# Three edits to an AdaLN and FFN kernel: one transfer for the small inputs, tap scalings on another engine, and x1's rows written in two later parts

## The chip, the cores and the metric

The kernel runs on one core of a Trainium2 chip. The metric is the device time of one execution in microseconds, as a median of several. A core has a matrix engine (TensorE, PE in the profile; its weight loads are PEld), a vector engine (VectorE, DVE), an activation engine (ScalarE, ACT), a general engine (GpSimd, POOL) and a queue engine (SyncE, SP). Each runs its own list of instructions in order. ACT, POOL and SP also issue the transfers, which 16 DMA engines carry out. Matrix results land in eight PSUM banks.

## The reference, cut to what matters

There are 32 images of 128 channels by 2048 positions. Two residual layers follow each other, `x = x + F0(x)` and `x = x + F1(x)`:

```python
# layer 0: a mixture of 8 1x1 convolutions per image, then a dense 2048x2048 layer with a low-rank update
h   = gelu(gelu(cond @ W0 + b0) @ W1 + b1)
att = softmax(h @ W2 + b2)                          # 32 x 8
y   = einsum('boi,bih->boh', einsum('bk,koi->boi', att, weight), x) + (att @ bias_k)[:, :, None]
x   = x + y @ W.T + bias + lowrank(y)
# layer 1: grouped convolution (4 groups, 9 taps, padding 4), then a block-wise FFN on permuted positions
y   = conv1d(x, w9, groups=4, padding=4) + (cond @ c_weight.T)[:, :, None] + fside[None, :, None]
t   = y.reshape(4096, 2048)[:, perm].reshape(4096, 16, 128)
t   = einsum('bhm,hmd->bhd', gelu(einsum('bhd,hdm->bhm', t, up)), down)
x   = x + t.reshape(4096, 2048)[:, unperm].reshape(32, 128, 2048)
```

All inputs and the result are float32.

## The kernel before

**The dense layer** is computed ahead of the mixture: the product of x with the 2048x2048 matrix comes first, the 128x128 mixtures of each image are applied to its result. It is done in seven rounds (`ROUNDS`, P1, P2, P6, P7, P5, P3, P4: a Strassen-like scheme on quarters of the matrix), each over eight groups `g` of four images. One round and group is one call of `multiply`: seven inner products, each of 4 matmuls (8 records in the profile), on three banks `px`, `py`, `pz`. After each product `add` puts the bank onto an accumulator, by ScalarE where the accumulator is new (L278) and by VectorE else (L276). Several products use the same bank one after the other, so the next product on `px` waits for the `add` of the last. Between two products `between(j)` puts other work into the queues. In round P1 this is the making of the matrix itself from W and the low-rank factors (`w_make`, L167, L171). In rounds P2 to P3 it is the mixing of the kernels of the images (`mixed_kernel`, L356, L358, VectorE). GpSimd makes sums of the inputs and weights for the coming products (L229 to L253, L336, L338).

**The small work** is a generator, `small()`, that is moved on by one piece after each `multiply`. Its first piece (L664 on) comes after the first multiply: ScalarE issues ten transfers of small inputs into one tile `small`, and then those of `perm` into `pos` and of the mixture's weights into `mix`. The following pieces compute the attention over the eight kernels. Later pieces (L770 to L793) transform the 9-tap convolution kernels: VectorE combines the three parts `T0`, `T1`, `T2` of `toep` to six sets of taps, four into `tw` and two in place, and SP stores them.

**The last round (P4) and the FFN** are run as one pipeline of stages `k`. Each `multiply` of the last round holds three stages, between its products; then each of the 128 heads of the FFN (eight groups by 16 heads: `ffn_up` L626, gelu L629, `ffn_down` L637, residual add L642, scatter L644) is one stage. A pair of images `c` takes 12 stages, n = -2 to 9, and a new pair starts every eight stages, so n of one pair is n - 8 of the next:

- n = -2 and 1: `mix_loads` of the pair's first and second image (SP: L365, L368, L373); n = -1 and 2: `mix_bias` (GpSimd: L379)
- n = 0 and 2: `mix_begin` (ScalarE: L387), `mix_work` (PE L396, VectorE L399); then SP moves the new x, called x1, channel group by channel group to two tiles `xg` (L403)
- n = 3: `residual_rows` (VectorE: 16 transposes, L436, into two tiles `x1t`, and two stores of 1024 KB by SP, L409)
- n = 4 and 5: `conv_inputs` (VectorE, L466 to L478) for the first half of the channels, n = 7 and 8 for the second
- n = 5, 6 and 8, 9: the convolution's products (`conv_begin`, `conv_middle`, `conv_end`, PE L487) and the rest of it, with `conv_rows` (8 transposes, L423, and two stores) at n = 6 and 9.

`xg` holds both images of a pair, as index `j`: j = 0 came at stage n = 0, j = 1 at n = 2. The gathers of a group of images (GpSimd, L610) read what `residual_rows` and `conv_rows` stored to `hx_d`. In the list of one stage the loads and biases come first, then `ffn_up`, the middle products, `ffn_down` of the head before, and at the end `stage_third`: products, then `third_rest` with the transposes and the inputs of the convolution. All orders are the program's own (`manual_schedule`). Tiles of 128x2048 come from a pool of 24 slots. Before a transfer by SP or ACT is issued it can have to wait for an earlier one whose semaphore it takes over: eight are dealt out in turn for both queues together.

Of the kernel before, what the change touches and what calls it, by code (L numbers as in the profile page):

```python
# [11 lines left out]
ALU = mybir.AluOpType  # L12
# [4 lines left out]
P = 128  # L17
B = 32
L = 2048
QW = 512  # L20
KEXP = 8
GR = 4
GC = 32
TAPS = 9
NPH = 4
NK = 4
NM = QW // NK
# [8 lines left out]

ROUNDS = ("P1", "P2", "P6", "P7", "P5", "P3", "P4")
# [3 lines left out]
def adaln_ffn_kernel(  # L45
# [1 line left out]
    tc: tile.TileContext,  # L47
    x: bass.AP,
    xT: bass.AP,
    condT: bass.AP,  # L50
    fside: bass.AP,
    W0: bass.AP,
    b0: bass.AP,
    W1: bass.AP,
    b1: bass.AP,
    W2: bass.AP,
    b2: bass.AP,
    mixT: bass.AP,
    bias_kT: bass.AP,
    WT: bass.AP,  # L60
    fbias: bass.AP,
    A: bass.AP,
    BfT: bass.AP,
    coeffs: bass.AP,
    toep: bass.AP,
    cwT: bass.AP,
    ffw: bass.AP,
    perm: bass.AP,
    out: bass.AP,
# [1 line left out]
    nc = tc.nc  # L71
# [271 lines left out]


    ags = {}
    late, ins, pms, xgs, va, vb, hts, open_ = {}, {}, {}, {}, {}, {}, {}, {}

    def mixed_kernel(b, ks):

# [57 lines left out]
    def store(c, o, h, t):  # L407
        g, j = c // 2, c % 2
        nc.sync.dma_start(  # L409
            hx_d[g][:, o, j * 2 * P : (j + 1) * 2 * P].rearrange(  # L410
                "(p h s) t -> p h s t", h=2, s=2 * NM // GC
            )[:, h],
            t.rearrange("p k s j r c -> p (k s) (j r c)"),
        )

    def rows_tile(name):
        return slot(name, (P, 2, NM // GC, 2, GR, GC))
# [7 lines left out]
                v[:, r].rearrange("p j (s c) -> p j s c", c=GC),  # L425
            )

    def residual_rows(c):

        ts = [rows_tile(f"x1t_{c}{h}") for h in range(2)]  # L430
        for j in range(2):
            for h, t in enumerate(ts):
                for k in range(2):
                    for i in range(2):
                        n0 = (2 * h + k) * NM
                        nc.vector.transpose(  # L436
                            t[:, k, :, j, 2 * i : 2 * i + 2].rearrange("p s r c -> p r s c"),
                            xgs[c][i][:, :, j, n0 : n0 + NM].rearrange("p r (s c) -> p r s c", c=GC),
                        )
        for h, t in enumerate(ts):  # L440
            store(c, 1, h, t)

# [141 lines left out]
    def third_rest(c, n):  # L586
        if n in (6, 9):
            conv_rows(c, int(n == 9))
        if n == 3:
            residual_rows(c)  # L590
        if n in (4, 5, 7, 8):
            conv_inputs(c, int(n > 5), n in (5, 8))
        if n == 8:
            xgs.pop(c)

# [70 lines left out]
    def small():  # L666
        sm = slot("small")
        used = [0]

        def load(name, src, rows, cols, eng=nc.scalar):  # L670
            t = sm[0:rows, used[0] : used[0] + cols]
            used[0] += cols
            if src is not None:
                eng.dma_start(t, src)
            return t

        cond_s = load("cond_s", condT, P, B)
        w0 = load("w0", W0, P, P)
        b0s = load("b0s", b0, P, 1)
        w1 = load("w1", W1, P, P)  # L680
        b1s = load("b1s", b1, P, 1)
        w2 = load("w2", W2, P, KEXP)
        b2s = load("b2s", b2.to_broadcast([B, KEXP]), B, KEXP)
        bk = load("bk", bias_kT, P, KEXP)
        cw = load("cw", cwT, P, GR * P)
        fb = load("fb", fside, P, GR)
        nc.scalar.dma_start(pos, perm)
        nc.scalar.dma_start(mix, mixT)
        h0, h1 = load("h0", None, P, B), load("h1", None, P, B)
        lg, ex, att = (load(n, None, B, KEXP) for n in ("lg", "ex", "att"))  # L690
        mx, su, rs = (load(n, None, B, 1) for n in ("mx", "su", "rs"))
        adiag = load("adiag", None, B, B * KEXP)
        ones = load("ones", None, P, P)
        nc.gpsimd.memset(ones, 1.0)
        yield

        p0 = bank()
        nc.tensor.matmul(p0[:, :B], lhsT=w0, rhs=cond_s, start=True, stop=True)
        nc.scalar.activation(h0, p0[:, :B], AF.Gelu, bias=b0s)
        done(p0)  # L700
        yield
        p1 = bank()
        nc.tensor.matmul(p1[:, :B], lhsT=w1, rhs=h0, start=True, stop=True)
        nc.scalar.activation(h1, p1[:, :B], AF.Gelu, bias=b1s)
        done(p1)
        yield
        p2 = bank()
        nc.tensor.matmul(p2[:B, :KEXP], lhsT=h1, rhs=w2, start=True, stop=True)
        nc.vector.tensor_tensor(lg, p2[:B, :KEXP], b2s, ALU.add)
        done(p2)  # L710
        nc.vector.tensor_reduce(mx, lg, AX.X, ALU.max)
        nc.vector.tensor_scalar(lg, lg, mx, None, ALU.subtract)
        nc.scalar.activation(ex, lg, AF.Exp)
        nc.vector.tensor_reduce(su, ex, AX.X, ALU.add)
        nc.vector.reciprocal(rs, su)
        nc.vector.tensor_scalar(att, ex, rs, None, ALU.mult)

        nc.vector.tensor_tensor(
            adiag.rearrange("b (c k) -> b c k", k=KEXP),
            ident.unsqueeze(2).to_broadcast([B, B, KEXP]),  # L720
            att.unsqueeze(1).to_broadcast([B, B, KEXP]),
            ALU.mult,
        )
        yield
        p3 = bank()
        nc.tensor.matmul(p3[:, : B * KEXP], lhsT=ones[0:B], rhs=adiag, start=True, stop=True)
        nc.vector.tensor_copy(att_bc, p3[:, : B * KEXP])
        done(p3)
        ab = att_bc.rearrange("p (b k) -> p b k", k=KEXP)
        nc.vector.tensor_scalar(aggb, ab[:, :, 0], bk[:, 0:1], None, ALU.mult)  # L730
        for k in range(1, KEXP):
            nc.vector.scalar_tensor_tensor(
                aggb, ab[:, :, k], bk[:, k : k + 1], aggb, ALU.mult, ALU.add
            )

        for r in range(GR):
            p4 = bank()
            nc.tensor.matmul(
                p4[:, :B], lhsT=cw[:, r * P : (r + 1) * P], rhs=cond_s, start=True, stop=True
            )  # L740
            nc.vector.tensor_scalar(ctxb[:, r], p4[:, :B], fb[:, r : r + 1], None, ALU.add)
            done(p4)
        nc.vector.tensor_scalar(ctx34, ctxb, 0.75, None, ALU.mult)

        nc.vector.tensor_scalar(row, pos, 3, 9, ALU.bitwise_and, ALU.logical_shift_left)
        nc.vector.tensor_scalar(
            orow[:, 0], pos, 0x1FC, None, ALU.bitwise_and
        )
        nc.vector.tensor_scalar(orow[:, 1], pos, 9, None, ALU.logical_shift_right)
        nc.vector.tensor_tensor(row, row, orow[:, 0], ALU.add)  # L750
        nc.vector.tensor_tensor(row, row, orow[:, 1], ALU.add)
        for g in range(NG):
            nc.vector.tensor_scalar(orow[:, g], pos, g * L, None, ALU.add)
        yield

        while len(made) < 16:
            yield
        wbc = slot("wbc", (P, NPH, QW))
        for o in range(NPH):
            p5 = bank()  # L760
            for half in (slice(0, NQ), slice(NQ, QW)):
                nc.tensor.matmul(
                    p5[:, half], lhsT=ones, rhs=wsum[:, o, half], start=True, stop=True
                )
            nc.scalar.copy(wbc[:, o], p5)
            done(p5)
        nc.sync.dma_start(w1_d, wbc.rearrange("p f n -> p (f n)"))
        yield


        tw, t1 = slot("tw", (P, 4, GR, P)), slot("t1", (P, 4, GR, P))
        nc.sync.dma_start(t1[:, 0:3], toep)
        yield
        yield
        T0, T1, T2 = (t1[:, i] for i in range(3))
        ts, stt = nc.vector.tensor_scalar, nc.vector.scalar_tensor_tensor
        nc.vector.tensor_tensor(tw[:, 1], T0, T2, ALU.add)
        ts(tw[:, 1], tw[:, 1], -1 / 6, None, ALU.mult)
        yield
        stt(tw[:, 0], T1, -1 / 6, tw[:, 1], ALU.mult, ALU.add)  # L780
        stt(tw[:, 1], T1, 1 / 6, tw[:, 1], ALU.mult, ALU.add)
        yield
        stt(tw[:, 3], T2, 4.0, T0, ALU.mult, ALU.add)
        ts(tw[:, 3], tw[:, 3], 1 / 12, None, ALU.mult)
        yield
        stt(tw[:, 2], T1, 1 / 6, tw[:, 3], ALU.mult, ALU.add)
        stt(tw[:, 3], T1, -1 / 6, tw[:, 3], ALU.mult, ALU.add)
        nc.sync.dma_start(tw_d, tw.rearrange("p k r c -> p (k r c)"))
        yield
        ts(T0, T0, 0.25, None, ALU.mult)  # L790
        ts(T1, T2, 4.0, None, ALU.mult)
        nc.sync.dma_start(te_d, t1[:, 0:2].rearrange("p k r c -> p (k r c)"))
        yield  # L793

# [54 lines left out]
    nxt, waiting, ts = {}, {}, {}  # L849
# [6 lines left out]
    for i, (r, g) in enumerate(steps):  # L856
# [17 lines left out]
        if ri == 0:  # L874
            for k in blocks[4 + 2 * g : 6 + 2 * g]:
                t = make(k)
# [6 lines left out]
        elif ri + 1 < len(ROUNDS):  # L883
# [3 lines left out]
            if 2 <= g < 6:  # L887
                k = ((g - 2) // 2, (g - 2) % 2)
# [123 lines left out]
```

## Time and profile before

| | us |
|---|---|
| median of 3 runs | 2667.38 (2661.07 to 2668.86) |
| profiled execution | 2668.65 |
| its span | 2666.5 |
| PE busy | 2632.8 (99%) |
| DVE busy | 1359.2 (51%) |
| POOL busy | 1080.3 (41%) |
| ACT busy | 532.4 (20%) |

The profiled execution took 2.15 us more than its span, and is 1.27 us above the median. PE is busy nearly all the time, at a granted clock of 0.995 over the run; its waits for other engines sum to a little over 20 us. Times in the timeline are counted from the start of the span. A row of the timeline has the start, the time it took, the engine and line, the operation, its tiles (out<-in) and sizes, the number of instructions merged into it, and in brackets how long the engine had been idle before it and what ended the wait.

### The profile page before, as it was taken

To read this page: it belongs to the slowest core of one execution; us is meant where nothing else is said; L and a number is where in the kernel's file an instruction comes from. 1 tells how busy PE (TensorE), PEld (TensorE's weight loads), DVE (VectorE), ACT (ScalarE), POOL (GpSimd) and SP (SyncE) were. 2 spreads that over 40 slices of the span, in tenths; PEclk is the share of its full clock that TensorE was granted. 3 is DMA by queue.
4 is the path that set the end of the run, shared out by engine and by line. 5 is a ranking of instruction groups with operands and counts; after the bars stand their busy time and mean duration, and the time that the engine had idled before them with its cause. 6 is when DMAs were issued, how large, how long until landed. Compare 5 with 4: busy or idle time off the path is not lost.

```text
span 2666.5 us, 19802 instructions
## 1 busy us (share of the span) xinstructions
PE 2632.8 (99%) x6504; PEld 1236.3 (46%) x6504; DVE 1359.2 (51%) x2136; ACT 532.4 (20%) x1099; POOL 1080.3 (41%) x665
## 2 busy tenths in 40 slices
PE   9999999999999999999999999999999999999998
PEld 4444444444444444444444445544555455555543
DVE  6545145233344355454266666666666666566610
ACT  0000100000000000000011144444444444444432
POOL 2544545624636421656242232434332343333222
PEclk9999999999999999999999999999999999999999
DMA  8876547445466366555577788777777877777532
GB/s 331 326 302 253 228 165 314 180 162 207 182 233 257 145 263 271 217 216 225 206 247 246 214 275 273 228 232 235 242 250 235 254 218 235 223 236 236 164 126 87
DMA packets 184534, 609.14 MB, mean 228 GB/s; under 512 B 17777, under 2 KB 88689, under 8 KB 140017
## 3 DMA queue, kind: packets, MB, share of 16 engines
q1 hardware_dynamic: 148656, 466.40, 49.6%
q0 software_dynamic: 34144, 140.53, 15.4%
q8 instruction: 52, 0.85, 0.1%
q10 hardware_dynamic: 1632, 0.96, 0.1%
q14 instruction: 50, 0.40, 0.0%
HBM read 364.03 MB, written 210.24 MB: 215 GB/s over the span
## 4 chain that ended last, share of the span: by engine, by line
PE 90%; DVE 4%; DMA 4%; POOL 1%; issue 0%; SPq 0%; ACTq 0%; POOLq 0%; ACT 0%; DVEq 0%
PE bank L283 46%; PE bank L626 16%; PE bank L637 16%; PE bank L487 6%; PE bank L396 4%; PE bank L167 2%; DVE ags L358 2%; DMA xt<-in_xT 1%; DMA bf_sb<-in_BfT 1%; DMA u<-u_d 1%; DMA xg<-x 1%; DVE u L276 0%; DVE vb L466 0%; DMA s_d<-xt 0%; DMA small<-in_W 0%
## 5 line engine op out<-in xcount | busy, mean ns | idle before, releaser
L626 PE MATMUL bank<-t,ws 128*128 128x512 f32 x1024 | 460.3, 592 | 0.0
L637 PE MATMUL bank<-gl,ws 128*128 128x512 f32 x1024 | 460.2, 592 | 0.0
L283 PE MATMUL bank<-P_t,s_P 128*128 128x512 f32 x896 | 397.0, 596 | 7.9 <-ACT m_P L278 4.2
L644 POOL DMA_INDIRECT out<-t,orow x128 | 153.0, 1195 | 616.7 <-DVE t L642 485.1
L629 ACT ACTIVATE gl<-bank 128x512 f32<-128x512 f32 x512 | 306.1, 598 | 455.1 <-PE bank L626 442.3
L276 DVE TENSOR_TENSOR u<-bank,u 128x512 f32<-128x512 f32 x280 | 187.1, 686 | 386.4 <-PE bank L283 377.4
L637 PEld LDWEIGHTS bank<-gl,ws 128*128 128x128 f32 x1024 | 194.6, 190 | 233.0 <-issue 231.3
L626 PEld LDWEIGHTS bank<-t,ws 128*128 128x128 f32 x1024 | 194.6, 190 | 226.8 <-issue 216.7
L283 PE MATMUL bank<-wo_P,s_P 128*128 128x512 f32 x640 | 283.3, 593 | 2.9 <-DVE u L276 2.9
L387 ACT ACTIVATE bank<-w,aggb 128x512 f32<-128x512 f32 x128 | 80.8, 684 | 999.9 <-DMA w<-w_d 981.8
L283 PEld LDWEIGHTS bank<-P_t,s_P 128*128 128x128 f32 x896 | 171.2, 192 | 224.4 <-issue 215.0
L642 DVE TENSOR_TENSOR t<-bank,t 128x512 f32<-128x512 f32 x128 | 88.0, 688 | 289.1 <-PE bank L637 268.9
L379 POOL TENSOR_TENSOR x<-x,fb 128x1024 f32<-128x1024 f32 x64 | 149.6, 2359 | 165.6 <-DMA x<-in_x 152.8
L276 DVE TENSOR_TENSOR p<-bank,p 128x512 f32<-128x512 f32 x112 | 77.4, 691 | 243.3 <-PE bank L283 243.2
L283 PEld LDWEIGHTS bank<-wo_P,s_P 128*128 128x128 f32 x640 | 120.9, 190 | 157.1 <-issue 146.4
L358 DVE SCALAR_TENSOR_TENSOR ags<-mix,att_bc,ags 128x128 f32<-128x128 f32 x224 | 177.2, 791 | 4.5
L283 PE MATMUL bank<-wo_P,xt 128*128 128x512 f32 x384 | 169.0, 592 | 0.0
L234 POOL TENSOR_TENSOR s_P<-xt 128x512 f32<-128x512 f32 x40 | 51.8, 1295 | 256.0 <-DMA xt<-in_xT 228.9
L283 PE MATMUL bank<-P_t,xt 128*128 128x512 f32 x320 | 147.0, 603 | 6.5 <-DVE u L276 6.5
L610 POOL DMA_INDIRECT t<-hx_d,row x128 | 124.9, 976 | 59.4 <-issue 26.6
L487 PE MATMUL bank<-va,tw_l 128*128 128x256 f32 x512 | 122.8, 382 | 3.3 <-DVE va L470 3.3
L399 DVE TENSOR_TENSOR x<-bank,x 128x512 f32<-128x512 f32 x128 | 85.9, 689 | 64.8 <-POOL x L379 29.7
(136 smaller groups left out, 2800.7 us busy)
## 6 DMA issues: line engine op xcount, KB each, us to landing
xt<-in_xT SPq DMA_DIRECT2D x64, 1024.0 KB
u<-u_d SPq DMA_DIRECT2D x40, 1024.0 KB
wo_P<-wb_d SPq DMA_DIRECT2D x36, 1024.0 KB
u<-c_d SPq DMA_DIRECT2D x64, 512.0 KB
x<-in_x SPq DMA_DIRECT2D x32, 1024.0 KB
xg<-x SPq DMA_DIRECT2D x256, 128.0 KB
hx_d<-x1t SPq DMA_DIRECT2D x32, 1024.0 KB
hx_d<-ht SPq DMA_DIRECT2D x32, 1024.0 KB
```

What stands on the lines that cost most here:

```text
L276: nc.vector.tensor_tensor(to, ps, to, ALU.add)
L283: nc.tensor.matmul(ps, lhsT=lhs[k][:, bass.ts(kc, P)], rhs=rhs[k][:, kc], start=first and kc == 0, stop=last and kc == 3, skip_group_check ...
L358: nc.vector.scalar_tensor_tensor(ag, mix[:, k], att, ag, ALU.mult, ALU.add)
L379: nc.gpsimd.tensor_tensor(xt[:, f : f + 2], xt[:, f : f + 2], late["fb"][:, f : f + 2], ALU.add)
L396: nc.tensor.matmul(pm, lhsT=ag, rhs=u[:, f], start=False, stop=True, skip_group_check=True)
L487: nc.tensor.matmul(out, lhsT=w[:, 2 * i + r], rhs=rhs, start=first and r == 0, stop=last and r == 1, skip_group_check=True,)
L610: nc.gpsimd.indirect_dma_start(out=t.rearrange("p k t -> p (k t)"), out_offset=None, in_=hx_d[g].rearrange("l k t -> l (k t)"), in_offset= ...
L626: nc.tensor.matmul(pu, lhsT=w[:, m * P : (m + 1) * P], rhs=t[:, 0], start=True, stop=True)
L629: nc.scalar.activation(gl[m], pu, AF.Gelu)
L637: nc.tensor.matmul(pd, lhsT=w[:, (MC + m) * P : (MC + m + 1) * P], rhs=gl[m], start=(m == 0), stop=(m == MC - 1),)
L642: nc.vector.tensor_tensor(t[:, 1], pd, t[:, 1], ALU.add)
L644: nc.gpsimd.indirect_dma_start(out=out, out_offset=bass.IndirectOffsetOnAxis(ap=orow[:, g, h : h + 1], axis=0), in_=t[:, 1], in_offset=None,)
```

## The change

The host lays the ten small inputs side by side in one array `smalls` of 128 rows, and one transfer brings it; `pos` and `mix` follow as before. Four scalings of the taps go from VectorE's `tensor_scalar` to ScalarE's `mul`. `residual_rows` is cut by image (j) and by half of the output (h): at n = 3 only the eight transposes of j = 0 are put out; those of j = 1 come at n = 4 (h = 0) and n = 5 (h = 1), four each, after `conv_inputs` of that stage; the store of each half comes right after its last transposes. The lines of the changed kernel shift; the matmuls, their order and the order of GpSimd's instructions stay as they are.

```diff
@@ residual rows
-    def residual_rows(c):
-
-        ts = [rows_tile(f"x1t_{c}{h}") for h in range(2)]
-        for j in range(2):
-            for h, t in enumerate(ts):
-                for k in range(2):
-                    for i in range(2):
...
-        for h, t in enumerate(ts):
-            store(c, 1, h, t)
+    def residual_rows(c, j, h):
+        if j == 0:
+            x1ts[c, h] = rows_tile(f"x1t_{c}{h}")
+        t = x1ts[c, h]
+        for k in range(2):
+            for i in range(2):
+                n0 = (2 * h + k) * NM
+                nc.vector.transpose(
+                    t[:, k, :, j, 2 * i : 2 * i + 2].rearrange("p s r c -> p r s c"),
+                    xgs[c][i][:, :, j, n0 : n0 + NM].rearrange("p r (s c) -> p r s c", c=GC),
+                )
+        if j == 1:
+            store(c, 1, h, x1ts.pop((c, h)))
@@ third_rest
         if n == 3:
-            residual_rows(c)
+            residual_rows(c, 0, 0)
+            residual_rows(c, 0, 1)
         if n in (4, 5, 7, 8):
             conv_inputs(c, int(n > 5), n in (5, 8))
+        if n in (4, 5):
+            residual_rows(c, 1, n - 4)
@@ small inputs
-        cond_s = load("cond_s", condT, P, B)
-        w0 = load("w0", W0, P, P)
...
-        fb = load("fb", fside, P, GR)
+        cond_s, w0, b0s, w1, b1s, w2, b2s, bk, cw, fb = (take(P, n) for _, n in SMALLS)
+        nc.scalar.dma_start(sm[:, 0 : used[0]], smalls)
         nc.scalar.dma_start(pos, perm)
         nc.scalar.dma_start(mix, mixT)
@@ taps
-        ts(tw[:, 1], tw[:, 1], -1 / 6, None, ALU.mult)
+        nc.scalar.mul(tw[:, 1], tw[:, 1], -1 / 6)
...
-        ts(tw[:, 3], tw[:, 3], 1 / 12, None, ALU.mult)
+        nc.scalar.mul(tw[:, 3], tw[:, 3], 1 / 12)
...
-        ts(T0, T0, 0.25, None, ALU.mult)
-        ts(T1, T2, 4.0, None, ALU.mult)
+        nc.scalar.mul(T0, T0, 0.25)
+        nc.scalar.mul(T1, T2, 4.0)
```

## Prediction

> **What bounds the kernel now.** First the busy shares of the page:
>
> ```profile
> span 2666.5 us, 19802 instructions
> PE 2632.8 (99%) x6504; PEld 1236.3 (46%) x6504; DVE 1359.2 (51%) x2136; ACT 532.4 (20%) x1099; POOL 1080.3 (41%) x665
> ```
>
> PE is the bound; the change touches no matmul, so it can win or lose only where PE stands still. Then the waits of PE (total, times, longest):
>
> ```profile
> PE bank L283 <- DVE u L276: 10.0, 9, 6.5
> PE bank L283 <- ACT m_P L278: 4.2, 1, 4.2
> PE bank L283 <- DVE p L276: 3.6, 3, 2.8
> PE bank L487 <- DVE va L470: 3.3, 3, 2.2
> ```
>
> The three longest, 6.5, 4.2 and 2.8 us, are single events. PE's timeline around each:
>
> ```profile
> 86.55 7.03 PE L283 MATMUL bank<-w,xt 128*128 128x512 f32 x16
> 97.75 8.66 PE L283 MATMUL bank<-P_t,s_P 128*128 128x512 f32 x16 [4.17 <-ACT m_P L278]
> 106.25 7.03 PE L283 MATMUL bank<-w,s_P 128*128 128x512 f32 x16
> ...
> 443.05 7.03 PE L283 MATMUL bank<-w,xt 128*128 128x512 f32 x16
> 452.90 8.58 PE L283 MATMUL bank<-P_t,s_P 128*128 128x512 f32 x16 [2.83 <-DVE p L276]
> 461.32 7.03 PE L283 MATMUL bank<-w,s_P 128*128 128x512 f32 x16
> ...
> 1521.61 7.03 PE L283 MATMUL bank<-wo_P,s_P 128*128 128x512 f32 x16
> 1535.18 6.74 PE L283 MATMUL bank<-P_t,xt 128*128 128x512 f32 x8 [6.54 <-DVE u L276]
> 1541.75 3.60 PE L626 MATMUL bank<-t,ws 128*128 128x512 f32 x8
> ```
>
> Undisturbed, 16 records go from start to start in 6.87 us (55.65 to 62.52), 8 in 3.43. So a stall costs more than its idle time, as the next matmuls are slow:
> - at 97.75: due 86.55 + 6.87 = 93.42, 4.33 late; then 106.25 - 97.75 = 8.50, 1.63 too long: **5.96**
> - at 452.90: due 449.92, 2.98 late; then 8.42, 1.55 too long: **4.53**
> - at 1535.18: due 1528.48, 6.70 late; then 6.57 for 8 records, 3.14 too long: **9.84**.
> A small one, at 1449.38 (due 1448.65, then 0.07 too long), costs 0.80. The windows show the granted clock at 0.83 from 97 to 107 and 0.55 from 1535 to 1542.
>
> What ended the waits, from the timelines of ACT and DVE:
>
> ```profile
> 93.13 1.01 ACTq L687 DMA_DIRECT2D pos<-in_perm  x1
> 97.02 0.58 ACT L278 COPY m_P<-bank 128x512 f32<-128x512 f32 x1 [23.42 <-DMA pos<-in_perm]
> ```
> ```profile
> 443.85 3.66 DVE L790 TENSOR_SCALAR t<-t 128x512 f32<-128x512 f32 x1
> 447.43 4.72 DVE L791 TENSOR_SCALAR t<-t 128x512 f32<-128x512 f32 x1
> ```
> ```profile
> 1522.42 2.72 DVE L436 STREAM_TRANSPOSE x1t<-xg 128x256 f32<-128x256 f32 x8
> 1530.69 0.45 DVE L436 STREAM_TRANSPOSE x1t<-xg 128x256 f32<-128x256 f32 x1 [5.55 <-DMA xg<-x]
> ```
>
> The first: ScalarE's copy of a bank stands behind twelve transfers that ScalarE issues from 81.97 to 96.9. The second: two scalings by VectorE. The third: the transposes of the second image wait for `xg`, and the `add` that frees PE's bank stands behind them. The 0.80 at 1449 is of this kind (3.41 us for `xg` at 1445).
>
> **What the Trainium skill says.** "TensorE: Matmul & The Clock Gate", section "What's actually happening": the array falls to half clock when idle and needs about 3.4 us of work to come back. The traced 1.55 to 3.14 us after each stall agree. "SBUF — State Buffer", section "Who interferes with whom": VectorE instructions in a two-port mode (`tensor_scalar` can be) or with two SBUF inputs and a GpSimd one that reads SBUF lock each other out. The trace agrees: L790 and L791 lie under GpSimd's L336 (442.72 to 447.23) and L338 (447.31 to 451.87), while L778, the same shape, took 0.43. ScalarE has ports of its own there.
>
> **Part 1, one transfer.** Twelve issues become three. The first still starts at 81.97, when its slot is freed (a store from 72.02 lands). The chain shows that before, `pos` waited 9.52 us for an earlier small transfer to land and `mix` 3.91 for another: semaphores taken over. With three, `pos` needs none of these and `mix` one of a load that landed long ago (its tile was used at 54.66). Issues of 0.3 to 1.9 us each end by about 86; the bank is ready at 90.2, due at PE at 93.42. Gain 5.96. The first reader of `small` runs at 116.55, 30 us later. SP loses two waits on small transfers (11.8 and 10.5 us) in front of x loads. VectorE and GpSimd had slack there (idle 11.6 and 11.5 us).
>
> **Part 2, scalings.** Four instructions leave VectorE (0.43, 0.51, 3.66, 4.72). On ScalarE they cost about 0.68 each (L387, same size) and hide: ScalarE waits 981.8 us in one piece between rounds P1 and P4. The store of `te` (SP waited 7.8 us for it) comes earlier. GpSimd's lock stays: the two `mixed_kernel` instructions next in line would now meet it from 447.3 to 451.9. The `add` PE waits for is ahead of them, at 446.7; the one after is due by 456.8. Gain 4.53. A stall of 0.6 at 425.80 (L787, stays on VectorE) remains.
>
> **Part 3, rows in halves.** The work is the same, 16 transposes of 0.34. In the last round there are three pairs:
> - c = 0: four more (1.36) stand before an `add` that PE takes from 1370.64; it would end at 1370.9, so **+0.4**.
> - c = 1: -0.80; `conv_inputs` and four transposes end at 1455.9, the next `add` is due at 1457.2.
> - c = 2: the two `add`s come at 1525.2 and 1528.7, PE goes on at 1528.48: -9.84. Now `conv_inputs` waits for `xg` (1530.69); its v[2] (L470) is ready after 4.4 us, at 1535.1, and `conv_begin` wants it at 1536.2. Slack 1.1 only.
>
> The cost is in SP's queue: the store of the second half now waits until n = 5, and `mix_loads` of the next pair stand behind it. In the period from 2037 both stores went at 2044.64 and x at
>
> ```profile
> 2050.54 1.49 SPq L373 DMA_DIRECT2D x<-in_x  x1
> ```
>
> Now the last transposes end at 2053.9 (conv inputs of before) + 0.4 + 1.36 = 2055.7, x goes at about 2060 (the five issues of 2086.79 to 2092.96 took about that) and lands 6.4 us after its issue (2020.24 to 2026.62): 2066.5. GpSimd's bias takes it at 2068.52 (its turn, it did not wait for x). If x is later, the bias (4.67, reads SBUF) slides under L466 of n = 7, which it stretches already:
>
> ```profile
> 2070.67 3.62 DVE L466 SCALAR_TENSOR_TENSOR vb<-xg 128x1024 f32<-128x1024 f32 x1
> ```
>
> Unstretched it takes 1.2. At 4.03 and 4.30 PE stood 0.40 and 0.67 for L470 (the waits at 1644.55 and 2367.29), at 3.62 not at all. So PE stands for what L466 takes over 3.63, and here x may land 2.0 us later than reckoned before a further microsecond costs one. The period from 2254 has 2.1. Thirteen pairs (c = 3 to 15, n = 3 at k = 8c - 18) are so placed. I take **+0.5** over all, bounds -1 (the two small stalls go) and +25. For the pair at the first heads the shift is larger, since the stall of 9.84 no longer covers it: behind store, `c_d`, two `ws`, store and u (6 MB at some 0.35 MB/us from 1537.3, with gathers between) x lands at about 1558, where the bias had its turn at 1560.41 - 9.84 = 1550.6; it would meet L469 and L470 there and cost 0 to 2.4: **+1.0**. The `ws` of the third head, due at 1547.4, goes at 1538.3 behind two stores of 1 MB: 1546.7, just in time, up to +3.
>
> **Sum.** -5.96 - 4.53 - 0.80 - 9.84 + 0.4 + 0.5 + 1.0 = -19.2 against the profiled 2668.65 (span 2666.5, 2.15 around it), that is 2649.4. The median of the runs is 1.27 lower: **2648**.
>
> **The rivals.**
> 1. *The wait for `xg` only moves.* `conv_inputs` needs the same data one stage later. For it: `xg` is late because of bandwidth (landing at 1530.69 from issues at 1513 to 1520), and slack is 1.1 us. Against: in the FFN `xg` landed before n = 4 began (1609 against 1612). Then part 3 gives 0 to 5 instead of 9: 2653 to 2657.
> 2. *Slower: SP's queue.* x lands late in every period, bias and `conv_inputs` collide, PE waits 13 times. It eats the gains of 21.1 - 1.4 when x comes 3.5 us later than reckoned (1.5 us in each period), and makes the kernel slower by over 0.3% from 4.1 us on. At 4.5 it gives 13 x 2.5 = 32 less 19.7: 2680. For it: bursts in which the DMA engines are 9 tenths busy, and 152.8 us that GpSimd already waits for x of the second images. Against: those come from a place that isn't changed, and 18 us lie between issue and use now.
> 3. *The transfer doesn't free ScalarE,* because `smalls` or `mix` still waits on the ring, or PE runs into a late x load next: part 1 gives nothing, 2654.
>
> **How the numbers follow.** Some 0.3% (8 us) is what a measurement of this kernel tells from no change. Main case, 2643 to 2653: 0.62. Rival 1: 0.18, a quarter of it with other losses within 0.3%. Rival 3: 0.08. Rival 2: 0.12, about half within 0.3% and half beyond. Faster (under 2659.4): 0.62 + 0.135 + 0.08 = 0.84; same 0.10, slower 0.06. The range 2642 to 2660 leaves out most of rival 2 and little more, and takes in the spread of the runs (0.15% either way).
>
> **What would show it.** Right: PE's table of waits without the rows for ACT m_P and DVE p (but for 0.4 to 0.8), the row for DVE u down from 10.0 to about 3, ScalarE's copy at 90.2, no transpose waiting for `xg` at j = 1, PE busy about 2626.5 (2632.8 less the slow matmuls, 1.63 + 1.55 + 3.14) in a span of about 2647. Wrong: a wait for `va` L470 in many periods with L466 above 3.6 us and GpSimd's L379 waiting for x in both images (rival 2), PE idle at 1530 to 1548 for `va`, `t` or `ws` (rival 1), a wait at 93 as before (rival 3).

## The result and the profile after

| | before | after |
|---|---|---|
| median | 2667.42 us (22 runs) | 2661.58 us (22 runs) |
| ratio of the runs | | 0.9983, 95% interval 0.9976 to 0.9990 |
| profiled execution, span | 2668.65, 2666.5 | 2658.77, 2657.0 |

The change makes the kernel 0.17% faster, some 4.5 us (2.7 to 6.4 by the interval). 19 us were predicted. The profiled execution of after lies 2.8 us below the median of its runs; the first experiments show where most of that may come from. First the busy shares of the page of after:

```profile
span 2657.0 us, 19770 instructions
PE 2630.5 (99%) x6504; PEld 1235.7 (47%) x6504; DVE 1369.3 (52%) x2132; ACT 535.2 (20%) x1103; POOL 1087.3 (41%) x665
```

PE is busy 2.3 us less than before; 6.3 had been expected. VectorE is busy 10 us *more*, although four scalings of 9.3 us in all left it: it was held up somewhere. The waits of PE (total, times, longest):

```profile
PE bank L484 <- DVE va L467: 7.1, 4, 4.2
PE bank L281 <- DVE u L274: 4.4, 8, 1.5
...
PE bank L281 <- DVE p L274: 1.4, 2, 1.0
PE bank L281 <- ACT m_P L276: 0.9, 1, 0.9
```

(L484, L467, L281, L274, L276 are L487, L470, L283, L276, L278 of before.) The three long single stalls are gone, as foreseen. In their place the wait for `va`, the convolution's inputs, has gone from 3.3 to 7.1. The timeline of PE at the places that matter:

```profile
95.30 7.11 PE L281 MATMUL bank<-P_t,s_P 128*128 128x512 f32 x16 [0.88 <-ACT m_P L276]
...
446.52 7.03 PE L281 MATMUL bank<-P_t,s_P 128*128 128x512 f32 x16
...
1395.86 1.43 PE L484 MATMUL bank<-va,tw_l 128*128 128x256 f32 x4 [4.22 <-DVE va L467]
...
1452.45 1.13 PE L484 MATMUL bank<-va,tw_l 128*128 128x256 f32 x4 [1.41 <-DVE va L467]
1455.05 5.10 PE L281 MATMUL bank<-wo_P,s_P 128*128 128x512 f32 x8 [1.47 <-DVE u L274]
...
1526.99 3.60 PE L281 MATMUL bank<-P_t,xt 128*128 128x512 f32 x8
```

446.52 and 1526.99 are the second and third stall of before: no bracket, no wait. At 95.30 something is left. 1395.86 had 2.22 before, and 1452.45 and 1455.05 had nothing. As PE does the same matmuls in the same order, one can subtract the start of each in before from its start in after. I call this difference the position of PE. It is negative where after is ahead, and where it changes, time is won or lost:

| stretch of before | position of after, from to | change | predicted |
|---|---|---|---|
| start to 60 | 0 to +0.84 | +0.84 | 0 |
| 97 to 106 (part 1) | +0.84 to -4.01 | -4.85 | -5.96 |
| 336 | -4.01 to -3.43 | +0.58 | 0 |
| 453 to 461 (part 2) | -3.43 to -7.94 | -4.51 | -4.53 |
| 1370 to 1407 (c = 0) | -7.94 to -5.50 | +2.44 | +0.4 |
| 1449 (c = 1) | -5.50 to -6.31 | -0.81 | -0.80 |
| 1456 to 1461 (c = 1) | -6.31 to -1.49 | **+4.82** | 0 |
| 1535 to 1542 (c = 2) | -1.49 to -11.33 | -9.84 | -9.84 |
| FFN to the end | -11.33 to -9.5 | +1.8 | +1.5 |

The two gains at 453 and 1535 came to within two hundredths of a microsecond. The large miss in this table is in c = 0 and c = 1. A second one, in part 1, it does not show, as it is a table of one execution only.

### The profile page after: what moved, and what is told of

It reads as the page before. It is cut to its first block, busy times and chain, and to the rows that moved or that the text cites. A ratio compares the mean times of both kernels' runs of the same rounds, so it can differ in the third digit from the quotient of the medians.

```text
span 2657.0 us, 19770 instructions
## 1 busy us (share of the span) xinstructions
PE 2630.5 (99%) x6504; PEld 1235.7 (47%) x6504; DVE 1369.3 (52%) x2132; ACT 535.2 (20%) x1103; POOL 1087.3 (41%) x665
## 4 chain that ended last, share of the span: by engine, by line
PE 91%; DVE 4%; DMA 3%; POOL 1%; issue 1%; SPq 0%; POOLq 0%; ACT 0%; DVEq 0%; ACTq 0%
PE bank L281 47%; PE bank L626 16%; PE bank L637 16%; PE bank L484 6%; PE bank L394 4%; PE bank L165 2%; DVE ags L356 2%; DMA bf_sb<-in_BfT 1%; DMA xt<-in_xT 1%; DVE va L464 0%; DVE vb L463 0%; DMA wb_d<-w 0%; DVE u L274 0%; DMA ws<-in_ffw 0%; DVE vb L466 0%
## 5 line engine op out<-in xcount | busy, mean ns | idle before, releaser
L281 PE MATMUL bank<-P_t,s_P 128*128 128x512 f32 x896 | 393.8, 592 | 1.3 <-ACT m_P L276 0.9
L274 DVE TENSOR_TENSOR u<-bank,u 128x512 f32<-128x512 f32 x280 | 187.3, 687 | 398.3 <-PE bank L281 389.2
L281 PE MATMUL bank<-wo_P,s_P 128*128 128x512 f32 x640 | 284.7, 596 | 4.4 <-DVE u L274 4.4
L281 PEld LDWEIGHTS bank<-P_t,s_P 128*128 128x128 f32 x896 | 170.1, 190 | 215.3 <-issue 214.8
L377 POOL TENSOR_TENSOR x<-x,fb 128x1024 f32<-128x1024 f32 x64 | 155.9, 2454 | 228.3 <-DMA x<-in_x 150.5
L274 DVE TENSOR_TENSOR p<-bank,p 128x512 f32<-128x512 f32 x112 | 77.3, 690 | 241.7 <-PE bank L281 241.7
L281 PEld LDWEIGHTS bank<-wo_P,s_P 128*128 128x128 f32 x640 | 121.5, 191 | 159.6 <-issue 149.5
L281 PE MATMUL bank<-wo_P,xt 128*128 128x512 f32 x384 | 169.0, 592 | 0.0
L281 PE MATMUL bank<-P_t,xt 128*128 128x512 f32 x320 | 144.0, 592 | 0.1
L484 PE MATMUL bank<-va,tw_l 128*128 128x256 f32 x512 | 123.0, 381 | 7.3 <-DVE va L467 7.1
L484 PEld LDWEIGHTS bank<-va,tw_l 128*128 128x128 f32 x512 | 96.7, 190 | 50.1 <-issue 38.0
```

Of the source, the lines that this page charges most:

```text
L274: nc.vector.tensor_tensor(to, ps, to, ALU.add)
L281: nc.tensor.matmul(ps, lhsT=lhs[k][:, bass.ts(kc, P)], rhs=rhs[k][:, kc], start=first and kc == 0, stop=last and kc == 3, skip_group_check ...
L377: nc.gpsimd.tensor_tensor(xt[:, f : f + 2], xt[:, f : f + 2], late["fb"][:, f : f + 2], ALU.add)
L484: nc.tensor.matmul(out, lhsT=w[:, 2 * i + r], rhs=rhs, start=first and r == 0, stop=last and r == 1, skip_group_check=True,)
```

## The experiments: each part alone

Three kernels take one part of the change each; a fourth takes it all, but for the pairs c = 0 and 1. The parts are those of the diff above.

**Part 1 alone** (one transfer):

> The kernel before with part 1 alone (one transfer for the small inputs). Theory A (each part does what its trace says; the losses sit in the last round): the stall at 97.75, 5.96 us in all before, shrinks to about 1 and nothing else moves, so about 5 us less, 2662.5 and a ratio of 0.998; PE's wait for ACT m_P stays at 0.9 because ScalarE's copy waits for a slot that a store by GpSimd (wb_d) frees. Theory B (part 1 gives nothing of its own): the wait is 4 us, ratio 1.000.

Measured: 2667.71 us, ratio 0.9997 (0.9989 to 1.0006), so no gain that can be measured. Theory A is wrong here, and so is my step. Its profile has a wait of PE for ACT m_P of 4.4 us, as long as before. The timeline of ScalarE shows why:

```profile
83.08 0.55 ACTq L675 DMA_DIRECT2D mix<-in_mixT  x1
97.47 0.58 ACT L276 COPY m_P<-bank 128x512 f32<-128x512 f32 x1 [23.62 <-DMA wb_d<-w]
```

The transfers are out at 83.6, as planned, and ScalarE is free for 14 us. But its copy writes a new tile `m_P`, and that tile's slot is given up by a tile of made weights only when GpSimd's store of it (`wb_d`) has landed. That store was issued at 83.54 and landed 13.8 us later. The chain of after has the same step, 12.11 us from 82.31. In before the store took 8.6 us from 83.40, so the slot came at about 92.0. With the copy (0.58) and 0.15 on each side of it, as in after (94.42 to 94.57, 95.15 to 95.30), PE could have gone at 92.9, ahead of its 93.42. So the slot was not what held PE before; the store takes longer now.

**Part 2 alone** (scalings on ScalarE):

> The kernel before with part 2 alone (four scalings of the taps on ScalarE). Theory A: the stall at 452.90 (4.53 us) goes whole, all others stay: ratio 0.9983. Theory B (GpSimd's sums then lock out the mixed_kernel instructions of VectorE that take the place of the scalings): a wait of 1 to 3 us stays near 453, ratio 0.999 to 1.000.

Measured: 2662.00, ratio 0.9978 (0.9971 to 0.9985). In its profile the position of PE goes from -3.70 to -8.30 at 453 to 461: -4.60. The ratio, 5.9 us less (4.0 to 7.7), agrees. Theory A stands. But this kernel has all twelve transfers, and still its wait for ScalarE's copy, at 95.6, is short:

```profile
PE bank L283 <- ACT m_P L278: 1.1, 1, 1.1
```

So that stall differs between executions of the same code. Its price in each profile (from the start of the product on w,xt to that on w,s_P, less 2 x 6.87) is with twelve transfers 5.97 (before), 1.36 and 4.34; with one transfer 1.12 (after), 6.32, 0.01, 8.20 and 2.61, taking in the kernels below (0.01 where PE had come 4.4 us late from the start). The means, 3.9 and 3.7, are alike. After's own profile, 1.12, lies 2.5 under its mean: that would be most of the 2.8 us by which it beats the median of its runs.

What the copy waits for is not alike. With twelve transfers it follows ScalarE's last issue (`mix` at 96.57, 94.42 and 95.13, the copy at 97.02, 94.87 and 95.59), and the store had landed by 92.0, after 8.6, 8.4 and 8.5 us. With one transfer it follows the store, which took 12.1, 13.8, 13.8, 15.1 and 12.8 us. What changed beside the store is SP's queue, here in part 2 alone (twelve) and then in part 1 alone (one):

```profile
85.72 11.40 SPq L202 DMA_DIRECT2D xt<-in_xT  x3
97.21 1.75 SPq L155 DMA_DIRECT2D w<-in_WT  x2
```
```profile
85.72 2.79 SPq L200 DMA_DIRECT2D xt<-in_xT  x3
88.60 15.67 SPq L153 DMA_DIRECT2D w<-in_WT  x2
```

With twelve, one load of x goes out and the next waits until 96.6 for a small transfer. With one, three loads of x and one of w, 1 MB each, are out by 89.7, while the store is under way. That these loads make the store longer fits all eight profiles, but no kernel here holds them back to test it.

**Part 3 alone** (rows in halves):

> The kernel before with part 3 alone (rows of x1 in halves, in all 16 pairs). Theory A: -9.8 at the end of the last round, -0.7 at 1449, but +2.4 at 1401, +4.7 at 1452 to 1461 and about +1.8 over the FFN, so 1.6 us less in sum, ratio 0.9994. Theory B (the losses come only together with parts 1 and 2, by the other dealing of semaphores or the earlier start): no waits over 2.5 us in the last round, 8 to 10 us less, ratio 0.9965.

Measured: 2665.50, ratio 0.9990 (0.9983 to 0.9996), 2.7 us less (1.1 to 4.5). The profile has all the places of theory A: +3.3 at c = 0, -0.8 and +4.95 at c = 1, -9.84 at c = 2. They do not depend on parts 1 and 2, so theory B is out. Over the FFN this execution, the slowest of its 21, lost 7.0 us.

**Halves from c = 2 on:**

```diff
         if n == 3:
-            residual_rows(c, 0, 0)
-            residual_rows(c, 0, 1)
+            for j in range(1 if c > 1 else 2):
+                residual_rows(c, j, 0)
+                residual_rows(c, j, 1)
...
-        if n in (4, 5):
+        if n in (4, 5) and c > 1:
             residual_rows(c, 1, n - 4)
```

> The changed kernel, but the pairs c = 0 and 1 have all their 16 transposes at n = 3 as before; halves from c = 2 on. Theory A (the losses are those of c = 0 and 1): PE's position against the kernel before stays at -7.9 from 461 to 1535 and goes to -17.8 there, then loses 1.8 in the FFN: 2652 in a profile, 6 to 7 us less than the changed kernel; its stalls at 1395 and 1449 are those of before (2.2 and 0.6). Theory B (the losses are those of the 14 later pairs and the FFN): no faster than the changed kernel, 2661.

Measured: 2656.13, ratio 0.9959 (0.9945 to 0.9972): 11 us less than before and 6 less than the changed kernel. From 461 to 1456 the position moves by -1.9 in all (-5.67 to -7.54), then by -9.84 at c = 2. Theory A: what was lost in the last round was lost at c = 0 and c = 1. (The FFN lost 4.9 here, not 1.8.)

## The experiments: why c = 0, c = 1 and the FFN lose

At c = 1 the timelines of VectorE and GpSimd in after, side by side:

```profile
1445.21 1.64 DVE L464 TENSOR_TENSOR va<-vb 128x512 f32<-128x512 f32 x1
...
1450.76 1.63 DVE L467 SCALAR_TENSOR_TENSOR va<-vb 128x512 f32<-128x512 f32 x1
```
```profile
1444.66 1.64 POOL L232 TENSOR_TENSOR s_P<-xt 128x512 f32<-128x512 f32 x1 [15.68 <-DMA xt<-in_xT]
...
1449.60 2.24 POOL L235 TENSOR_TENSOR s_P<-xt,s_P 128x512 f32<-128x512 f32 x1
```

VectorE's 128x512 instructions take 1.64 us where they take 0.69 in before (L467, 1451.19), and GpSimd's 1.27 become up to 2.24. This is the lock of "SBUF — State Buffer", section "Who interferes with whom", as in the prediction: each locks the other out of a port pair. L463 to L468 took 9.0 us instead of 5.1. In before the same four sums ran at 1460.62, after `conv_inputs`. Why they are earlier stands in the queue of SP. The load that they wait for (`xt`) in before and in after:

```profile
1446.78 1.67 SPq L409 DMA_DIRECT2D hx_d<-x1t  x2
...
1450.05 1.20 SPq L202 DMA_DIRECT2D xt<-in_xT  x1
```
```profile
1437.64 0.38 SPq L200 DMA_DIRECT2D xt<-in_xT  x1
```

In before the two stores of `x1t` stood ahead of it, waiting for the transposes. The change moved these stores behind it. The load went 12.4 us earlier while PE there was only 6.2 ahead, and GpSimd's sums slid under `conv_inputs`. The test puts the load back without touching the halves:

```diff
+        held = last_round and g == 5
         if i + 1 < len(steps):
-            if i + 1 not in xs:
+            if i + 1 not in xs and not held:
                 xs[i + 1] = x_loads(*steps[i + 1])
...
+                if j == 3 and held:
+                    xs[i + 1] = x_loads(*steps[i + 1])
```

> The changed kernel, but the load of x for the last group (L200, at 1437.64 in its profile) is issued two stages later, behind the store of the first half of c = 1, so that GpSimd's sums (L232 to L235) cannot run at 1444 to 1452. Theory A (these four sums, 6.8 us of GpSimd under conv_inputs of c = 1, are what stretched L464 to L467): L463 to L468 take about 5.1 us again instead of 9.0, the waits of 1.41 and 1.47 at 1452 and 1455 go, PE's position gains 4 to 5 us there: 2657, ratio to the kernel before 0.9965. Theory B (the four transposes added to the stage are what is late): the wait for va goes at most in part and the wait for u L274 stays, gain under 2 us.

Measured: 2659.55, ratio 0.9970 (0.9958 to 0.9982). VectorE and PE in its timeline:

```profile
1452.90 0.69 DVE L464 TENSOR_TENSOR va<-vb 128x512 f32<-128x512 f32 x1
...
1455.49 0.69 DVE L467 SCALAR_TENSOR_TENSOR va<-vb 128x512 f32<-128x512 f32 x1
...
1457.71 1.89 PE L484 MATMUL bank<-va,tw_l 128*128 128x256 f32 x8
```

Both waits are gone, and PE's position gains 4.8 us there over after. Theory A; the four added transposes cost nothing here. The run times alone would not decide it, as this interval overlaps that of the changed kernel. (At the start this execution was the worst, 8.20: its `wb_d` took 15 us.)

At c = 0 it is the other transfer: x for the mixing. Its issue came 10.35 us after PE's product at 1363.02 began; in before 7.92 after the same product. So GpSimd's bias (L377) ran at 1383.98 to 1389.6, under L463 and L464, which took 2.86 and 2.72 (before: 1.92 and 1.64). This is rival 2. In before and in after:

```profile
1388.24 4.66 POOL L379 TENSOR_TENSOR x<-x,fb 128x1024 f32<-128x1024 f32 x2 [23.04 <-DMA x<-in_x]
...
1392.06 1.92 DVE L466 SCALAR_TENSOR_TENSOR vb<-xg 128x1024 f32<-128x1024 f32 x1
1394.02 1.64 DVE L467 TENSOR_TENSOR va<-vb 128x512 f32<-128x512 f32 x1
```
```profile
1383.98 5.63 POOL L377 TENSOR_TENSOR x<-x,fb 128x1024 f32<-128x1024 f32 x2 [27.92 <-PE bank L281]
...
1384.56 2.86 DVE L463 SCALAR_TENSOR_TENSOR vb<-xg 128x1024 f32<-128x1024 f32 x1
1387.45 2.72 DVE L464 TENSOR_TENSOR va<-vb 128x512 f32<-128x512 f32 x1
```

To test it, x goes first in its group of loads:

```diff
     def mix_loads(b):
         g, tp, s = b // GB, b % GB // 2, b % 2
+        xt = slot(f"x_{b}", (P, NPH, QW))
+        nc.sync.dma_start(xt.rearrange("p f n -> p (f n)"), x[b])
         ag = agp.tile([P, P], FP, name=f"agl_{b}", tag="ag")
...
-        xt = slot(f"x_{b}", (P, NPH, QW))
-        nc.sync.dma_start(xt.rearrange("p f n -> p (f n)"), x[b])
```

> The changed kernel, but mix_loads issues the load of x ahead of those of agl and u instead of behind them. Theory A (PE's waits for va come from x being late, so that GpSimd's bias runs under conv_inputs): x goes some 2 to 4 us earlier, the bias mostly ends before L463, the wait of 4.2 us at 1395 falls to 2 or less, and the loss over the FFN, 1.8 us in this kernel's profile, 7.0 and 5 in the two others with part 3, falls to 1 or less: 3 to 6 us less, ratio to before 0.996 to 0.997. Theory B (the later stores and transposes themselves delay PE, or u now comes late): no gain, ratio 0.998 or more, with waits of PE L394 for u.

Measured: 2655.43, ratio 0.9961 (0.9946 to 0.9975), 10 us less than before, with a wait of 2.08 at c = 0. PE's position gains 1.8 us at c = 0 where after lost 2.4. At c = 1 it loses 1.5 for 4.8: GpSimd's four sums start 2 us later there, at 1446.61, and stretch fewer instructions. How long GpSimd's bias waited for x in all (total, times, longest), in before, in after, in part 3 alone and with x first:

```profile
POOL x L379 <- DMA x<-in_x: 152.8, 16, 24.5
```
```profile
POOL x L377 <- DMA x<-in_x: 150.5, 21, 24.6
```
```profile
POOL x L379 <- DMA x<-in_x: 206.4, 25, 26.2
```
```profile
POOL x L377 <- DMA x<-in_x: 92.8, 7, 24.5
```

After's total is no larger than that of before, but it has more waits, and two others of 50.4 us in all, the one at 1383.98 among them, are put down to PE. The FFN, from PE's first matmul on t,ws to its last end: 1115.2 to 1116.8 in the four profiles without part 3 (mean 1115.9, the last one below); 1117.0, 1122.2, 1120.1, 1117.3 and 1118.6 with it (mean 1119.0); 1116.0, 1115.8 and 1118.1 with x first (mean 1116.6). So part 3 costs the FFN some 3 us, twice what I had put, and the order of the four loads gives most of that back. With x first PE waits for `va` once, 0.8 us at the first heads, and nowhere later; with part 3 alone there are five such waits of 0.4 to 1.8 from 1714 on.

## The experiments: the start, and the parts together

If the slot of `m_P` is what is late, an earlier store must help. In round P1 GpSimd's sums (`x_outer`, four of 4.5 us) stood ahead of two stores of made weights:

```diff
             if not last_round:
                 lhs[i + 1] = x_combine(*steps[i + 1], xs.pop(i + 1))
-                x_outer()
+                if ri > 0:
+                    x_outer()
...
                 t = make(k)
+                x_outer()
```

(and once more after the loop over the blocks).

> The changed kernel, but in round P1 GpSimd's sums for the outer products (x_outer, 19 us with their stores) stand behind the first of the two stores of the made weights (wb_d) instead of ahead of both. Theory A (with three transfers instead of twelve, ScalarE's copy at 94 to 97 still waits for the slot that this store frees): the store goes at about 64 instead of 82 to 83.5, the copy comes about 3.6 us after the product on w,xt starts (91), PE's wait for ACT m_P goes whole: 1 to 4 us less than the changed kernel, ratio to before 0.997 to 0.998. Theory B (the copy waits for something else, a late x or a busy DMA ring): the wait for m_P stays at 0.9 to 4.4.

Measured: 2657.98, ratio 0.9964 (0.9952 to 0.9977). The store goes at 60.05, and the timeline of ScalarE shows the copy in time, with no wait of PE:

```profile
74.89 1.82 ACTq L677 DMA_DIRECT2D mix<-in_mixT  x1
91.46 0.59 ACT L276 COPY m_P<-bank 128x512 f32<-128x512 f32 x1 [17.64 <-DMA s_d<-xt]
```

The small inputs go 7 us earlier too. Then the same edit without any part of the change:

> The kernel before with one edit: in round P1 the store of the first made weights stands ahead of GpSimd's sums for the outer products. The twelve transfers of small inputs stay twelve. Theory A (the late slot was what held ScalarE's copy at 97, and the slot of the tile small comes free earlier too): the twelve issues start near 73 and end before 91, the copy comes at 91, PE's wait for ACT m_P (4.2 in the profile of before) goes: about 4 us less, ratio 0.998, without any part of the change. Theory B (the number of transfers does it): the issues run past 91, PE waits 1 to 4 us for ACT m_P still, ratio 0.999 to 1.000.

Measured: 2663.04, ratio 0.9990 (0.9982 to 0.9997), 2.7 us less. ScalarE's timeline:

```profile
88.25 1.35 ACTq L688 DMA_DIRECT2D mix<-in_mixT  x1
93.40 0.59 ACT L278 COPY m_P<-bank 128x512 f32<-128x512 f32 x1 [16.62 <-PE bank L283]
```

The twelve issues start at 76.3 instead of 82.0, end at 89.6, and nothing waits for them. (In this execution, the slowest of its 17, PE had come 3.2 us late from the start; 89.6 is ahead of the 90.2 of before too.) Theory A: the stall at 97 goes without the one transfer, and the one transfer leaves it. With the store first the place costs 0.00, 0.57, 0.21 and 0.01 us in the four profiles that have it.

**Together.** First halves from c = 2 on, store first and x first:

> Halves from c = 2 on only, the store of the first made weights ahead of the outer sums, and the load of x first in mix_loads, together. If the causes are as in theory A of each, the savings add: ratio 0.9959 of the kernel with halves from c = 2 on, less 1 to 3 us at the start and 2 to 4 us in the FFN: 2650 to 2653, ratio 0.994 to 0.995. If they are not, no better than 0.9959.

Measured: 2650.16, ratio 0.9938 (0.9925 to 0.9951). The savings add up. Then the same with halves from c = 1 on and the load held:

> The kernel with all three edits (halves from c = 2, store first, x first), but halves from c = 1 on and the load of x for the last group held two stages. In the profile of that kernel c = 1 stands 2.16 us at 1439 for u, as its transposes wait for xg. Theory A (with the sums held back, the halves of c = 1 cost nothing): the wait goes, 2 to 3 us less than that kernel, 2647 to 2648, ratio to before 0.9928. Theory B (conv_inputs of c = 1 is stretched by something else, or the held load makes P_t,xt late): no gain, ratio 0.9938 or more.

Measured: 2647.96, ratio 0.9927 (0.9913 to 0.9940), 19 us less than before and 14 less than the changed kernel. The wait of 2.16 is gone, but in this execution the first heads gave 2.2 back (a wait for `va` of 1.46, one for `ws` of 1.12); against the kernel just before the two intervals overlap. The ratio to before is what theory A gave. The page of it:

```profile
PE 2624.7 (99%) x6504; PEld 1233.0 (47%) x6504; DVE 1352.1 (51%) x2132; ACT 535.4 (20%) x1103; POOL 1082.1 (41%) x665
```

VectorE is busy 17 us less than in after, with as many instructions; fewer of them met GpSimd's. In after 120 of them took over 1.3 times what others of their form take, every one with a GpSimd instruction beside it; here 106.

## Why the prediction was wrong

- **Part 1, -5.96: the step that failed.** "The bank is ready at 90.2, due at PE at 93.42" priced the bank and the issues, and not the tile that the copy *writes*. That hung on a store of GpSimd, and the store did not keep its time: 8.4 to 8.6 us with twelve transfers, 12.1 to 15.1 with one. The two waits that SP loses "in front of x loads" were listed and not followed. The copy came at 94.57 in after and at 97.47 with part 1 alone, and the part measured -0.8 us (-2.9 to +1.6) on its own. Of the 4.85 us that the two profiles show, most is the luck of two executions. Rival 3 named the outcome, by another cause (a late x).
- **Part 2, -4.53: right.** -4.51 in after and -4.60 alone. The named cover held: GpSimd's lock delayed nothing that PE waits for.
- **c = 2, -9.84: right,** three times to a tenth. `conv_inputs` waited 1.36 us for `xg` (1529.24), and PE did not wait, so rival 1 did not come.
- **c = 1, -0.80: the saving came (-0.81), and +4.82 with it.** I had gone through what the four transposes delay on VectorE. I had not asked what the *removed* stores let through on SP: a load 6 us earlier against PE, and by it GpSimd's sums into `conv_inputs`. For this stage "-0.80" should have been about +4.
- **c = 0, +0.4: mis-sized,** +2.44 in after and +3.3 with part 3 alone. The transposes' 0.4 was seen (1363.02), the late x was not.
- **FFN and first heads, +1.5: right mechanism, too small.** +1.8 in after, about +3 over five profiles, up to 7.0. `ws` cost 0.48 where 0 to 3 had been given.

With the terms as found, -0.8 - 4.6 + 2.4 + 4.0 - 9.8 + 3 = -5.8; measured were -4.5, 2.7 to 6.4. Of the signs named, three held (no wait for `xg` at j = 1, DVE p only twice and at most 1.0, DVE u at 4.4 for 3), and three did not: PE busy 2630.5 for 2626.5, the copy at 94.57 for 90.2, a row for ACT m_P. What stays open is whether it is SP's loads that lengthen `wb_d`. The kernels with the store first speak for it: their other `wb_d`, put out at 82.3 to 84.0, took 10.7 us with twelve transfers and 13.0 to 13.7 with one. And the parts alone add to 9.4 us less, 4.9 more than they gave together; that is a little more than the intervals leave to chance, and no run here explains it.

## What to carry to other kernels

When a wait is removed, list every other thing that the waiting instruction needs, the slot it writes included, with its time: the stall shrinks only to the next of them. When an instruction leaves a queue, ask what was held back behind it, when that will now run, and with whom it shares a port or the DMA engines. And read a stall in more than one execution before pricing it: one of 6 us here was 1.4 and 4.3 in two others with the same code at that place.

## What was not expected of the hardware

- From 84 to 100 us the DMA engines moved 424 to 429 GB/s in after, all engines busy. "DMA: Bandwidth & Descriptors", section "Where 436 GB/s comes from", puts the ceiling of the ports at 435.2 GB/s, and the trace stays just under it. The same section has some 358 GB/s as what binds transfers between HBM and SBUF; these loads and stores went faster. At this time the store of 1024 KB took from 8.4 to 15.1 us; put out 20 us earlier, 4.15 to 4.17 in all four profiles.
- Under a GpSimd instruction at c = 0 and 1, VectorE's two-input instructions took 1.63 to 2.72 us for 0.69 (128x512) and 1.8 to 2.9 for 1.22 (128x1024), while transposes under one kept their 0.34 each. With the order of transfers VectorE's busy time went from 1369 us (after) to 1352 (the last kernel).
- Equal stalls of PE did not cost the same. The same product in part 3 alone and with x first:

```profile
96.32 8.80 PE L283 MATMUL bank<-P_t,s_P 128*128 128x512 f32 x16 [2.40 <-ACT m_P L278]
```
```profile
97.19 7.10 PE L281 MATMUL bank<-P_t,s_P 128*128 128x512 f32 x16 [2.37 <-ACT m_P L276]
```

  The first lost another 1.77 us in slow matmuls (the next product came at 104.96, 8.64 later instead of 6.87), the second 0.07. And after the stall of 6.54 us in before, matmuls ran 0.85 us apart instead of 0.43 for 6.1 us (1535.18 to 1541.31). That is longer than the "about 3.4 us of work" with which the prediction found it in agreement.
